# A list scheduler's model of transfers: one serial line, or two queues that share the memory path, with new durations, in a fused graph-attention kernel

## The chip, the cores and the metric

One core of a Trainium2 chip runs the whole problem in one launch. The metric is the device time of that core in microseconds, the median of three runs. Beside it stands one profiled execution, from which all views come.

## The reference

For each of 32 graphs of 512 nodes: a layer norm and a ReLU over the 512 features, two graph-attention layers, and the input added back. Cut to what matters:

```python
h = jnp.maximum(_layernorm(x, axis=-1), 0.0)
def gat_layer(x, mask, W, a_src, a_dst, bias, concat):
    xl = (x @ W).reshape(B, N, H, F)
    asrc = jnp.einsum('bnhf,hf->bnh', xl, a_src)
    adst = jnp.einsum('bnhf,hf->bnh', xl, a_dst)
    e = jax.nn.leaky_relu(asrc[:, :, None, :] + adst[:, None, :, :], NEG_SLOPE)
    e = jnp.where(mask[..., None], e, NEG_INF)
    attn = jax.nn.softmax(e, axis=1)
    out = jnp.einsum('bsdh,bshf->bdhf', attn, xl)
    ...
mask = (adj > 0) | jnp.eye(N, dtype=bool)[None]
h = jax.nn.elu(gat_layer(h, mask, W1, att_src1, att_dst1, b1, concat=True))
return x + gat_layer(h, mask, W2, att_src2, att_dst2, b2, concat=False)
```

Layer 1 has 4 heads of 256 features, layer 2 one head of 512. All matmuls are in float32.

## The kernel before, in words

**Work.** The graphs are pipelined by hand in the main program: while graph i is in its second layer, graph i+1 is in its first, graph i+2 is projected and graph i+3 is loaded. Matrix products of 2 x 2 blocks are made from seven block products in place of eight (`sevens`, `gather1`, `gather2`), so there are block sums on VectorE ahead of them (`hs`, `t`, and sums in place in `ht`, `h1`, `p`) and copies or additions out of PSUM behind each (`minus`, `elu`).

The softmax of a head takes two passes. In the first (`Soft.first`) the scores with destinations on the partitions go through ScalarE (`l<-as,z`), VectorE adds the mask and takes the extreme (`l<-l,mt`), ScalarE takes exponentials and their sum (`l<-l,low`) and a logarithm. `spread` turns the few resulting columns into rows on all partitions, by a small transpose on VectorE and two transfers through DRAM on SyncE: `drr<-rr` and `rr<-drr` (`das<-as` and `as<-das` for the scores themselves). In the second (`Soft.second`) VectorE forms the logits `p<-rr,z`, GpSimd issues two accumulating DMAs that add the mask (`p<-dm`), and ScalarE takes the exponentials (`p<-p,z`). Only then can TensorE gather. The last graph's two late heads use the place of the first weights (`pz`, shown as `w_sb`).

**Transfers.** SyncE issues all plain loads and stores, the broadcasts through DRAM and the transposing DMAs (masks at L527, graph activations at L586). GpSimd issues the accumulating ones at L390, and takes a small power for the layer norm at L546. Each issue waits in its engine's own instruction order.

**Order.** Nothing is emitted while the program is written down. `Program.add` records jobs: engine, cost in microseconds, what they wait for, how to emit them, and for a transfer a size, which is its time on the memory path at full speed. Buffers and PSUM banks are given out in this recording, in program order. `Program.order` then looks for an order of each engine's jobs. `backwards` places the jobs from the end, which gives ranks. `forwards` runs the program in the planner's own time: at each step `next_job` gives the engine that can start first, and of its ready jobs the one of lowest rank. TensorE's jobs are taken from a queue in program order. Twelve rounds of both are made, the best end is kept, and `sooner` then improves stretches of 80 TensorE jobs. At last each job is emitted in the order found. All ScalarE work is issued from line L379, VectorE's from L382, SyncE's from L385, GpSimd's accumulations from L390, matmuls from L396.

**The planner's transfers before.** One line for both queues: a transfer starts when its issue has ended and 0.8 us have passed, or when the one before it has landed; it takes its size, and its readers are released 2.0 us later. No job of SyncE or GpSimd starts while more than 3.5 us (`AHEAD`) of transfers are ahead:

```python
if jobs[j][4] is not None:
    landed = max(landed, t + jobs[j][1] + self.DMA_LEAD) + jobs[j][4]
...
if e in ("SP", "POOL"):
    t = max(t, hold)
```

Of the kernel before, what the change touches and what calls it, by code (L numbers as in the profile page):

```python
# [19 lines left out]
P = 128  # L20
# [24 lines left out]
class Program:  # L45
# [9 lines left out]
    DMA_LEAD, DMA_TAIL, AHEAD = 0.8, 2.0, 3.5  # L55
# [28 lines left out]
    def forwards(self, rank):  # L84

        jobs, after = self.jobs, self.after
        n = len(jobs)
        cause = [None] * n
        left = [len(job[2]) for job in jobs]
        ready_at, start, landed = [0.0] * n, [0.0] * n, 0.0  # L90
        free, soon, ready = defaultdict(float), defaultdict(list), defaultdict(list)
        tensor = deque(j for j in range(n) if jobs[j][0] == "PE")
        for j in range(n):
            if not left[j] and jobs[j][0] != "PE":
                heappush(soon[jobs[j][0]], (0.0, j))
        done = []
        while len(done) < n:
            j, t = self.next_job(rank, free, soon, ready, tensor, left, ready_at, landed - self.AHEAD)
            start[j] = t
            free[jobs[j][0]] = t + jobs[j][1]  # L100
            done.append(j)
            if jobs[j][4] is not None:
                landed = max(landed, t + jobs[j][1] + self.DMA_LEAD) + jobs[j][4]
            for s in after[j]:
                if jobs[j][4] is not None:
                    r = landed + self.DMA_TAIL
                else:
                    r = t + jobs[j][1] + self.latency(j, s)
                if r > ready_at[s]:
                    ready_at[s], cause[s] = r, j  # L110
                left[s] -= 1
                if not left[s] and jobs[s][0] != "PE":
                    heappush(soon[jobs[s][0]], (ready_at[s], s))
        return start, done, cause
# [18 lines left out]
    def backwards(self, rank):  # L133

        jobs = self.jobs
        n = len(jobs)
        left = [len(s) for s in self.after]
        ready_at, start, moving = [0.0] * n, [0.0] * n, 0.0
        free, soon, ready = defaultdict(float), defaultdict(list), defaultdict(list)
        tensor = deque(j for j in reversed(range(n)) if jobs[j][0] == "PE")  # L140
        found = [j for j in range(n) if not left[j]]
        todo = n
        while True:
            for j in found:
                if jobs[j][4] is not None:
                    moving = max(moving, ready_at[j]) + jobs[j][4]
                    ready_at[j] = moving + self.DMA_LEAD
                if jobs[j][0] != "PE":
                    heappush(soon[jobs[j][0]], (ready_at[j], j))
            if not todo:  # L150
                return start
            j, t = self.next_job(rank, free, soon, ready, tensor, left, ready_at)
            start[j] = t
            free[jobs[j][0]] = t + jobs[j][1]
            todo -= 1
            found = []
            for d in jobs[j][2]:
                later = self.DMA_TAIL if jobs[d][4] is not None else self.latency(d, j)
                ready_at[d] = max(ready_at[d], t + jobs[j][1] + later)
                left[d] -= 1  # L160
                if not left[d]:
                    found.append(d)

    def next_job(self, rank, free, soon, ready, tensor, left, ready_at, hold=0.0):

        best = None
        for e in ("PE", "ACT", "DVE", "POOL", "SP"):
            if e == "PE":
                if not tensor or left[tensor[0]]:
                    continue  # L170
                t = max(free[e], ready_at[tensor[0]])
# [6 lines left out]
            if e in ("SP", "POOL"):  # L178
                t = max(t, hold)
            if best is None or t < best[0]:  # L180
                best = (t, e)
        t, e = best
        if e == "PE":
            return tensor.popleft(), t
# [3 lines left out]
        return heappop(ready[e])[1], t  # L188
# [3 lines left out]
    def order(self):  # L192
# [8 lines left out]
        for j in reversed(range(n)):  # L201
            later = self.DMA_LEAD + self.DMA_TAIL + (jobs[j][4] or 0.0)
# [54 lines left out]
def tile_gat(  # L257
# [159 lines left out]
    def weights1():  # L417
        for c in range(2):
            for r in range(2):
                for k in range(KQ):  # L420
# [3 lines left out]
                        0.75, (), [("w1", ix, k)], w1_sb[:, ix, k, :, 2:],  # L424
# [72 lines left out]
    def load(b):  # L497
        XT[b] = []
        for t in range(NT):
            xk, xt = xs.take()  # L500
            dma(0.75, (), [xk], xt, x[b, t * P : (t + 1) * P, :])
            XT[b].append((xk, xt))

    def masks(b):

        for t in range(NT):
            ak, a = adjs.take()
            dma(0.75, (), [ak], a, adj[b, t * P : (t + 1) * P, :])
# [8 lines left out]
            0.5, every, every, nc.vector.tensor_max,  # L517
# [3 lines left out]
        dma(0.45, every, [mk], md.rearrange("p t n -> p (t n)"), m.rearrange("p t n -> p (t n)"))  # L521
        tk, mt = mts.take()

        for t in (0, 2):
# [6 lines left out]
                1.25,  # L531
# [23 lines left out]
    def norm_turn(b, t):  # L555
# [19 lines left out]
        else:  # L575
# [13 lines left out]
                1.27,  # L589
# [16 lines left out]
    class Soft:  # L606
# [7 lines left out]
        def spread(self, v, keys, rows, to, through, n=NT):  # L614
# [8 lines left out]
                0.12, keys, [ok], nc.vector.transpose,  # L623
# [3 lines left out]
                0.03, [ok], [dk], dr[:k].rearrange("k (b j) -> b k j", j=32),  # L627
# [6 lines left out]
                0.18 * rows * n, [dk], [ok], o[:, :rows, : n * P],  # L634
# [77 lines left out]
        def second(self, h):  # L712
# [9 lines left out]
            for d0, d1, rk, rr in self.rr.pop(h):  # L722
# [16 lines left out]
                if not here:  # L739
                    mk, md = MASK[self.b]  # L740
                    for us in (0, 1), (2, 3):
                        keys = p_keys(pk, us)
                        accumulate(
                            2.2, keys + [mk], keys,
# [358 lines left out]
    def residual(b, places=(ts_,) * NT):  # L1103

        XR[b] = []
        for d in range(NT):
# [6 lines left out]
            dma(0.75, [x2_key(b, 0, 0)], halves, xr, x[b, d * P : (d + 1) * P, :])  # L1113
# [29 lines left out]
    def gather2(b, soft, blocks, order=LAST):  # L1143
# [4 lines left out]
        def put(n, u, bk, ps):  # L1148
# [7 lines left out]
            if n == 4 or r == 0 and upper[u[0]] == 0:  # L1156
                upper[u[0]] = -1
                dma(0.75, [xk, xk + (0,), xk + (1,)], (), out[b, d * P : (d + 1) * P, :], xt)
# [10 lines left out]
    def gather2_plain(b, soft):  # L1169
# [3 lines left out]
        for d in range(NT):  # L1173
# [9 lines left out]
            dma(0.75, [xk], (), out[b, d * P : (d + 1) * P, :], xr)  # L1183
# [169 lines left out]
```

## Time and profile before

| | us |
|---|---|
| median of three runs | 2785.93 |
| lowest and highest | 2783.84, 2788.35 |
| span of the profiled execution, first to last instruction | 2778.8 |
| the same execution: TensorE busy | 2746.2 |
| VectorE busy | 2645.4 |
| ScalarE busy | 2304.3 |
| GpSimd busy | 324.7 |
| share of the 16 DMA engines: SyncE's queue, GpSimd's queue | 43.6%, 25.2% |

The span counts from the first to the last instruction; the runs' times also hold what lies around it, so the median stands 7.1 us above this span. "Busy" is time in which an engine's instruction ran; PEld is the loading of weights into TensorE, which overlaps its matmuls. "Idle before" is the time for which an engine stood still ahead of an instruction, put down to the event that ended it. A granted clock of 1.00 is full speed of TensorE. Names read out<-in, without buffer numbers; `mm` is a PSUM bank, `w_sb` a weight (or what later takes its place).

### The profile page before, as it was taken

The page shows a single profiled execution, that of the slowest core. Times are in us where ns is not written, and L with a number is a line of the kernel's source. Part 1 is how long each engine was busy: PE and PEld are TensorE (multiplying, and loading weights), DVE is VectorE, ACT ScalarE, POOL GpSimd, SP SyncE. Part 2 cuts the span into 40 slices and gives each one's busy share as a digit, 9 for nine tenths or more (in the row PEclk, how much of TensorE's full clock was granted, in tenths as well). Part 3 has the DMA queues.
Part 4 walks back from the last instruction along what each step waited for, and adds up shares of the span by engine and source line. Part 5 has one row for each costly group of instructions (what it writes and reads, how often), then busy time and mean ns, then how long its engine had stood idle before and what let it go on. Part 6 is the DMA issues. An engine that isn't in the chain of part 4 may idle for free. (4 is left out here: it accounts for less than half of the span.)

```text
span 2778.8 us, 41571 instructions
## 1 busy us (share of the span) xinstructions
PE 2746.2 (99%) x12520; PEld 2373.9 (85%) x12520; DVE 2645.4 (95%) x6726; ACT 2304.3 (83%) x4870; POOL 324.7 (12%) x356
## 2 busy tenths in 40 slices
PE   7999999999999999999999999999999999999999
PEld 6688888888888888888888888888888888888887
DVE  7999999999999999999999999999999999998997
ACT  5988888889888888888888888888888888887883
POOL 0110111001111101111011101011110111101110
PEclk9999999999999999999999999999999999999999
DMA  7766767667777667676677766777666867678663
GB/s 228 171 176 178 201 174 199 171 175 181 191 194 174 179 165 203 177 186 184 172 192 184 196 168 175 178 189 195 183 175 175 202 166 202 157 189 182 169 158 107
DMA packets 370964, 501.55 MB, mean 180 GB/s; under 512 B 222260, under 2 KB 226868, under 8 KB 370740
## 3 DMA queue, kind: packets, MB, share of 16 engines
q1 hardware_dynamic: 324948, 332.16, 43.6%
q0 software_dynamic: 45792, 166.74, 25.2%
q8 instruction: 100, 1.64, 0.2%
q14 instruction: 124, 1.02, 0.1%
HBM read 315.89 MB, written 51.31 MB: 132 GB/s over the span
## 5 line engine op out<-in xcount | busy, mean ns | idle before, releaser
L396 PE MATMUL mm<-w_sb,hs 128*128 128x257 f32 (+2 forms) x3032 | 688.5, 381 | 4.9 <-DVE hs L382 2.5
L396 PEld LDWEIGHTS mm<-w_sb,hs 128*128 128x128 f32 x3032 | 575.8, 190 | 92.0 <-ACT xl L379 4.6
L390 POOL DMA_DIRECT2D p<-dm x314 | 276.2, 887 | 2346.3 <-DVE p L382 1600.3
L379 ACT ACTIVATE l<-as,z 128x512 f32<-128x512 f32 x640 | 442.8, 721 | 101.9 <-DMA as<-das 96.2
L379 ACT ACTIVATE l<-l,low 128x512 f32<-128x512 f32 x640 | 459.2, 721 | 49.1 <-DVE low L382 46.0
L396 PE MATMUL mm<-w_sb,ht 128*128 128x258 f32 x2112 | 481.4, 382 | 1.9 <-DVE xl L382 1.4
L396 PE MATMUL mm<-p,xl 128*128 128x256 f32 (+1 forms) x1984 | 468.0, 384 | 1.0 <-DVE h L382 0.8
L396 PE MATMUL mm<-w_sb,h 128*128 128x257 f32 x2056 | 467.8, 379 | 0.0
L379 ACT ACTIVATE p<-p,z 128x512 f32<-128x512 f32 (+1 forms) x636 | 427.2, 716 | 42.6 <-DMA p<-dm 28.1
L382 DVE SCALAR_TENSOR_TENSOR p<-rr,z 128x512 f32<-128x512 f32 (+1 forms) x636 | 449.0, 743 | 11.8 <-DMA rr<-drr 11.6
L396 PEld LDWEIGHTS mm<-w_sb,ht 128*128 128x128 f32 x2112 | 400.9, 190 | 61.8 <-DVE xl L382 4.1
L382 DVE CUSTOM_DVE_ANT_1 l<-l,mt 128x512 f32<-128x512 f32 x640 | 429.1, 685 | 12.0 <-ACT l L379 9.5
L396 PEld LDWEIGHTS mm<-w_sb,h 128*128 128x128 f32 x2056 | 389.4, 189 | 57.8 <-issue 0.5
L396 PEld LDWEIGHTS mm<-p,xl 128*128 128x128 f32 x1984 | 377.1, 190 | 61.7 <-issue 5.7
L379 ACT ACTIVATE xl<-mm 128x258 f32<-128x258 f32 (+2 forms) x748 | 279.8, 382 | 70.6 <-PE mm L396 68.7
L379 ACT ACTIVATE h<-mm 128x256 f32<-128x256 f32 x496 | 181.7, 378 | 91.0 <-PE mm L396 88.4
L382 DVE TENSOR_TENSOR xl<-xl,mm 128x258 f32<-128x258 f32 x558 | 222.8, 420 | 29.1 <-PE mm L396 24.3
L379 ACT ACTIVATE xr<-h,b_sb 128x512 f32<-128x512 f32 x248 | 176.7, 721 | 75.7 <-DVE h L382 72.0
L396 PE MATMUL mm<-t,hs 128*128 128x256 f32 x992 | 226.0, 380 | 2.9 <-ACT h L379 2.9
L396 PEld LDWEIGHTS mm<-t,hs 128*128 128x128 f32 x992 | 188.4, 190 | 29.9 <-ACT h L379 4.7
L382 DVE SCALAR_TENSOR_TENSOR h<-h,b_sb,xr 128x512 f32<-128x512 f32 x248 | 182.9, 747 | 3.2 <-ACT xr L379 3.1
L382 DVE TENSOR_TENSOR t<-mm,t 128x256 f32<-128x256 f32 (+1 forms) x424 | 172.8, 419 | 11.7 <-PE mm L396 10.5
(114 smaller groups left out, 3421.8 us busy)
## 6 DMA issues: line engine op xcount, KB each, us to landing
p<-dm POOLq DMA_DIRECT2D x314, 512.0 KB, 5.2
rr<-drr SPq DMA_DIRECT2D x159, 512.0 KB
x<-in_x_dram SPq DMA_DIRECT2D x129, 256.0 KB
adj<-in_adj_dram SPq DMA_DIRECT2D x128, 256.0 KB
as<-das SPq DMA_DIRECT2D x64, 512.0 KB
t<-in_x_dram SPq DMA_DIRECT2D x124, 256.0 KB
out_dram<-t SPq DMA_DIRECT2D x124, 256.0 KB
dm<-m SPq DMA_DIRECT2D x32, 512.0 KB
```

Of the source, the lines that this page charges most:

```text
L379: prog.add("ACT", cost, reads, writes, lambda: nc.scalar.activation(*a, **k))
L382: prog.add("DVE", cost, reads, writes, lambda: f(*a, **k))
L390: lambda: nc.gpsimd.dma_start(to, at, accum_op=OP.add), size,
L396: f(*a, **k)
```

## The change

It is all in the planner and in the numbers that the planner is given. No operation, buffer or wait is added or removed.

- Transfers of SyncE and of GpSimd wait in two queues (`wires`). The first of each moves at speed 1.0 when it is alone. When both move, SyncE's advances at 0.44 and GpSimd's at 0.62; with a transposing DMA (size `TURN`, 0.95) on SyncE, at 0.30 and 0.62.
- The time ahead of a transfer is 0.6 us (SyncE) and 0.75 us (GpSimd), before 0.8; the time after it 1.2 us, before 2.0.
- `AHEAD` stays 3.5 us but counts for each queue by itself (`behind`).
- `next_job` no longer takes the job; `take` does, after `step` has let the transfers that end earlier release their readers.
- Other sizes: mask store `dm<-m` 0.45 to 1.8; broadcasts 0.18 to 0.24 a row of 128; accumulations 2.2 to 2.3; transposes 1.25 and 1.27 to 0.95; small stores 0.03 to 0.2; loads 0.75 to 0.8 or 0.9; stores of the result 0.75 to 0.65. Two costs on VectorE: the diagonal of the mask 0.5 to 0.35, the small transpose 0.12 to 0.13.

The core of the diff:

```diff
-    DMA_LEAD, DMA_TAIL, AHEAD = 0.8, 2.0, 3.5
+    DMA_LEAD, DMA_TAIL, AHEAD = {"SP": 0.6, "POOL": 0.75}, {"SP": 1.2, "POOL": 1.2}, 3.5
+    ALONE = {"SP": 1.0, "POOL": 1.0}
+    SHARED = {0: {"SP": 0.44, "POOL": 0.62}, 1: {"SP": 0.3, "POOL": 0.62}}
+    TURN = 0.95
...
+        wires, now, behind = {"SP": deque(), "POOL": deque()}, 0.0, {"SP": 0.0, "POOL": 0.0}
...
-            j, t = self.next_job(rank, free, soon, ready, tensor, left, ready_at, landed - self.AHEAD)
-            start[j] = t
-            free[jobs[j][0]] = t + jobs[j][1]
-            done.append(j)
-            if jobs[j][4] is not None:
-                landed = max(landed, t + jobs[j][1] + self.DMA_LEAD) + jobs[j][4]
...
+        def step(until):
+
+            nonlocal now
+            busy = [q for q in wires if wires[q] and wires[q][0][1] <= now]
+            speed = self.ALONE
+            if len(busy) == 2:
+                speed = self.SHARED[jobs[wires["SP"][0][0]][4] == self.TURN]
+            event, which = until, None
+            for q in wires:
+                if wires[q]:
+                    j, since, todo = wires[q][0]
+                    t = now + todo / speed[q] if q in busy else since
+                    if t < event:
+                        event, which = t, q
+            for q in busy:
+                wires[q][0][2] -= (event - now) * speed[q]
+                behind[q] -= (event - now) * speed[q]
+            now = event
+            if which in busy:
+                j = wires[which].popleft()[0]
+                release(j, lambda s: event + self.DMA_TAIL[which])
+            return which is not None
+
+        while len(done) < n:
+            hold = {q: now + behind[q] - self.AHEAD for q in wires}
+            found = self.next_job(rank, free, soon, ready, tensor, left, ready_at, hold, now)
+            if step(found[0] if found else float("inf")):
+                continue
+            t, e = found
+            j = self.take(e, t, rank, soon, ready, tensor)
+            start[j] = t
+            free[e] = t + jobs[j][1]
+            done.append(j)
+            if jobs[j][4] is not None:
+                wires[e].append([j, free[e] + self.DMA_LEAD[e], jobs[j][4]])
+                behind[e] += jobs[j][4]
+            else:
+                release(j, lambda s: t + jobs[j][1] + self.latency(j, s))
...
-            if e in ("SP", "POOL"):
-                t = max(t, hold)
+            t = max(t, hold.get(e, 0.0), now)
...
-        dma(0.45, every, [mk], md.rearrange("p t n -> p (t n)"), m.rearrange("p t n -> p (t n)"))
+        dma(1.8, every, [mk], md.rearrange("p t n -> p (t n)"), m.rearrange("p t n -> p (t n)"))
...
-                0.18 * rows * n, [dk], [ok], o[:, :rows, : n * P],
+                0.24 * rows * n, [dk], [ok], o[:, :rows, : n * P],
...
-                            2.2, keys + [mk], keys,
+                            2.3, keys + [mk], keys,
```

## The prediction

> **What bounds the kernel now.** I read the page's busy shares first, then the waits of TensorE, then busy time by stretch of time, then the matmuls in order of time.
>
> ```profile
> span 2778.8 us, 41571 instructions
> PE 2746.2 (99%) x12520; PEld 2373.9 (85%) x12520; DVE 2645.4 (95%) x6726; ACT 2304.3 (83%) x4870; POOL 324.7 (12%) x356
> ```
>
> TensorE is busy all but 2778.8 - 2746.2 = 32.6 us. A busy TensorE is not always a fast one, so I counted records: the seven stretches of 100 us from 200 to 900 us hold 462 or 463 matmuls each, one every 216 ns; nothing is hidden in them. Idle time, by stretch: 11.5 us before the first matmul, 3.8 us after the last (the last addition and store), 5.2 us between 12 and 175 us, 12.1 us after 900 us. These lines show the waits that end last:
>
> ```profile
> PE mm L396 <- ACT x L379: 11.8, 2, 11.5
> PE mm L396 <- DVE hs L382: 3.9, 4, 2.2
> PE mm L396 <- ACT h L379: 3.1, 5, 1.6
> PE mm L396 <- ACT xl L379: 2.4, 4, 1.0
> PE mm L396 <- ACT w_sb L379: 2.2, 1, 2.2
> PE mm L396 <- ACT p L379: 1.7, 2, 1.2
> ```
>
> No line names a DMA: each wait is for a VectorE or ScalarE instruction, and a transfer reaches TensorE only through these. In the next view the columns are length, busy time (count) of PE, PEld, DVE, ACT and POOL, granted clock, DMA share, GB/s:
>
> ```profile
> 45.00:50.00 5.00, 2.52 (x13) 1.72 (x11) 4.44 (x15) 5.00 (x14) 0.00 (x0) 0.99 0.85 257
> 50.00:55.00 5.00, 5.00 (x16) 4.12 (x17) 5.00 (x19) 4.89 (x14) 0.00 (x0) 0.67 0.98 345
> 1060.00:1130.00 70.00, 67.31 (x308) 57.74 (x307) 65.77 (x162) 57.30 (x119) 5.17 (x6) 1.00 0.63 161
> 2500.00:2550.00 50.00, 47.82 (x218) 40.90 (x217) 45.21 (x117) 42.77 (x87) 8.34 (x9) 1.00 0.83 169
> 2680.00:2712.00 32.00, 28.32 (x121) 23.64 (x120) 31.15 (x70) 23.32 (x47) 3.45 (x4) 0.95 0.58 149
> ```
>
> The idle time sits in a few knots: at 45 us TensorE waits for VectorE's block sums `hs` (2.18 us); near 1080 and 1117 to 1120 us; near 2524 us; near 2690 us for the last graphs' `pz`. The second row has a price that idle time doesn't show: after the 2.48 us of idle the clock is 0.67, and 5 x 0.33 = 1.7 us are lost in matmuls at a lower clock.
>
> **What the Trainium skill says.** "Perfetto Trace Analysis", section Identifying the Most-Contended Engine, warns against matmul busy time and wants the share of weight loads: here 85%, with 216 ns between matmuls in each undisturbed stretch, which agrees that TensorE is the bound. "DMA: Bandwidth & Descriptors", section Issuing engines are not separate DMA queues, says that transfers of SyncE and GpSimd run on the same 16 engines and interleave: the page has both queues there (43.6% and 25.2%), so the new model's premise fits the trace. "TensorE: Matmul & The Clock Gate", section What's actually happening, says that an idle window of about 3.4 us halves the clock until a busy one; the trace has 0.67 after a shorter idle time.
>
> **The change, part by part.** It edits no operation, only the list scheduler's model of transfers. TensorE's jobs are taken from a queue in program order in both versions, so its sequence of 2,690 matmul groups and their 2746 us stay. What moves, in the two programs as emitted: 5,264 of 6,020 VectorE instructions have another place, 3,251 of 4,229 on ScalarE, 772 of 1,262 transfers on SyncE, 64 of 350 jobs on GpSimd. So the change can win at most what idle time is left (17.3 us between first and last matmul, some 3 us of lowered clock), and can lose more.
>
> My measure of a move: add the profiled durations of all that now stands ahead of an instruction on its engine, less what stood there before. That is how much later it comes if its engine has no idle time, so for ScalarE (17% idle) it is an upper value. A matmul group is late by this shift less its slack, the time between the end of its last producer and its own start (2.0 us at the median, under 1.04 us for one in ten).
>
> *Start, 44 to 175 us.* The softmax of graph 0 is put ahead of graph 1's projection. Of ScalarE's two copies `ht<-mm` that release TensorE at 45.72 us, the later one has eleven softmax instructions more and one copy less ahead: 4 x 0.61 + 6 x 0.71 + 0.2 - 0.3 = +6.6 us, with ScalarE 100% busy there. The two groups that follow take 1.9 us, so the next group would start at 45.72 + 6.6 + 1.9 = 54.2 us; it waits for `hs<-ht`, 14 places later on VectorE by 5.0 us, so at 49.90 + 5.0 = 54.9 us. Idle time merges with the 2.18 us there: net +5.0 us. For the clock I add 0.5 us (0 if it recovers as before, 1.7 if the longer idle time costs as much again). Graph 2's statistics and activations move from 94-131 us to about 50-68 us: six ScalarE instructions, some 5 us, which fit where ScalarE idled (2.6 us in 75-80 us, 1.5 in 55-60 us and the time that its copies now wait for the late matmuls). On SyncE one mask transpose (1.27 us) now stands ahead of graph 2's loads, and w2's loads follow later; TensorE first reads w2 at 104 us, over 50 us after its load was issued. On GpSimd the power of 1.0 us comes ahead of the first accumulation, which still waits for `rr` at 66 us. With TensorE 5.5 us late and its producers not, the later gaps 0.66 + 0.29 + 0.47 + 1.01 = 2.4 us are covered. Start: +5.5 - 2.4 = **+3.1 us**. If all ScalarE shifts up to 9.9 us (at 98.6 us) bite, +9.9.
>
> *Relief after 900 us.* The producers behind most gaps move ahead: by 3.9 to 6.2 us at 1080 to 1120 us (2.79 us of gaps), 3.1 us at 2524 us (2.18), 2.4 us at 2613 us (0.33), 5.2 us at 2711 us (0.67). At 2690 us the `pz` writes move up 6 to 8 places, and their accumulation, 4.85 us from issue to use, can start sooner (3.01 us of gaps and 0.05 x 32 = 1.6 us of clock). With the small ones at 946 and 2309 us (0.25 + 0.36): 11.2 us. Gaps of 1.08 us at 1798 us and 0.69 at 2437 us stay, as their producers don't move ahead. I take three quarters: **-8.4 us**; bounds -5.5 and -11.2.
>
> *New lateness after 200 us.* In some 17 places a producer moves later than its slack covers; the largest of each place add up to 9.6 us (1.75 at 909 us, 1.7 at 2746 us, else under 1). Idle time of VectorE and ScalarE ahead of them takes part of it: I take 0.4, **+3.8 us**; bounds 0 and 9.6.
>
> *End.* Two residual additions `t<-t,b_sb`, at 2762 and 2763 us before, now stand ahead of the first `p<-rr` of the last graph (2759.18 us), and so wait for their loads in front of it; the last 14 us of matmuls wait for that `p`. VectorE's 0.81 us of idle time at 2758-2759 us takes part of their 2 x 0.6 us, a late load adds: **+1.2 us**, bounds 0 and 3.
>
> Sum: 3.1 - 8.4 + 3.8 + 1.2 = -0.3 us. The profiled span 2778.8 would become 2778.5 us; the median of the runs lies 7.1 us above that span, and I keep this distance: 2785.9 - 0.3 = 2785.6, so **2786 us**.
>
> **Rivals.** *Faster.* The new places are covered, as each of TensorE's neighbours idles for 3 to 17%, and all relief comes: 3.1 - 11.2 + 1.2 = -6.9, 2779 us. For it: producers move ahead by more than the gaps they caused. Against: the delay at 45 us rests on an order that is certain.
>
> *Slower: waits at the head of VectorE's queue.* Its instructions wait in order. One pulled ahead of its transfer stops all behind it, copies out of PSUM and block sums first, and TensorE behind these. Place: once in each graph of the steady part, where loads, `rr` and accumulations are now believed to land at other times. Price: loads of `x` are first used 2.3 us after issue at the earliest and 4.8 us at the lower quartile; one taken at the early end and landing at the other makes 2.5 us, less the median slack of 2.0: 0.5 us x 26 graphs = 13 us, 2799 us. It decides from the point where such a wait exceeds 2 us. For it: VectorE has only 2 to 3 us of idle time in 100. Against: now VectorE waits only 29 us for DMA in the whole span.
>
> *Nothing changes* (the orders are the same) is excluded by the emitted programs.
>
> **Chances.** Some 0.2% (5.6 us) is what a measurement of this kernel can tell from no change: same is 2780.4 to 2791.5 us. Forecast (same) 0.38; faster 0.28; slower 0.34, with the uncovered start (+9.9) counted there. The bounds are -8 (all relief, no new lateness, no loss at the end) and about +17 us; 8 times in 10 the time lies between 2777 and 2800 us.
>
> **What would show it.** TensorE busy 2746 us again; a gap of 6 to 7 us in its matmuls at 45 to 55 us; no gap at 1080 to 1120 and 2524 us, and less at 2690 us; new gaps of a microsecond near 909 and 2746 us. I am wrong if the gap at 45 us is missing, or if idle time is spread over all graphs with VectorE waiting for DMA.

## The result, and the profile after

| | before | changed kernel |
|---|---|---|
| median of 15 runs each, us | 2785.93 | 2791.45 |
| lowest and highest, us | 2775.58, 2793.31 | 2786.52, 2803.51 |
| ratio, 95% interval | | 1.0029 [1.0017, 1.0042] |

The changed kernel is slower by 0.29%: 8.1 us (4.7 to 11.7), if the ratio is taken of 2785.9. (The ratio uses all runs; the two medians alone differ by 5.5 us.) The forecast was 2786 us and no measurable change, which it set at 2780.4 to 2791.5 us. The time lies inside by 0.05 us, and the interval shows a small loss all the same.

First the page of the changed kernel. Its lines of code stand 39 further down: matmuls are L435, ScalarE L418, VectorE L421, SyncE L424, GpSimd L429.

```profile
span 2787.2 us, 41515 instructions
PE 2749.1 (99%) x12520; PEld 2371.6 (85%) x12520; DVE 2643.1 (95%) x6726; ACT 2303.0 (83%) x4870; POOL 323.6 (12%) x356
```

The span is 8.4 us longer: 2.9 us more of busy TensorE and 5.5 us more of idle TensorE (2787.2 - 2749.1 = 38.1, before 32.6). Its waits (total, times, longest):

```profile
PE mm L435 <- ACT x L418: 10.8, 1, 10.8
PE mm L435 <- DVE hs L421: 8.1, 7, 3.4
PE mm L435 <- ACT ht L418: 5.0, 1, 5.0
PE mm L435 <- ACT xl L418: 3.6, 7, 1.0
PE mm L435 <- ACT h L418: 1.7, 2, 1.4
```

Two waits are new in size: one of 5.0 us for ScalarE's `ht`, and `hs`, 8.1 us in place of 3.9. The same five stretches as before (length, busy time of PE, PEld, DVE, ACT, POOL, granted clock, DMA share, GB/s):

```profile
45.00:50.00 5.00, 0.25 (x1) 0.25 (x2) 4.63 (x15) 5.00 (x13) 0.00 (x0) 0.99 0.94 257
50.00:55.00 5.00, 5.00 (x16) 4.07 (x16) 3.97 (x14) 3.13 (x10) 1.46 (x1) 0.67 1.10 297
1060.00:1130.00 70.00, 70.00 (x325) 61.26 (x323) 67.75 (x170) 62.00 (x131) 8.53 (x10) 1.00 0.73 188
2500.00:2550.00 50.00, 50.00 (x233) 43.70 (x232) 48.72 (x127) 42.65 (x85) 7.45 (x8) 1.00 0.81 197
2680.00:2712.00 32.00, 29.88 (x136) 25.23 (x135) 30.05 (x69) 24.89 (x55) 6.91 (x8) 1.00 0.85 215
```

The gap at 45 us is there (5.0 us in one piece, where 6 to 7 were named), the gaps at 1080 to 1120 and at 2524 us are gone, the one at 2690 us has shrunk. Two named signs did not come: TensorE is busy 2749.1 us and not 2746 again, and there are no gaps of a microsecond near 909 and 2746 us. The relief came, and the kernel is slower all the same. So I compared the start of each matmul group in the two traces: how late TensorE is against before. It is 2.4 us late at 228 us, 8.0 at 300, 11.4 at 900, 7.2 at 1125, 8.5 at 1780, 16.8 at 2380, 9.1 at 2712 and 8.4 at the end. What was forecast as relief came (-4.2 and -7.7 us); what was not forecast is the size of the new lateness between, some 19 us where 3.8 were expected.

The largest new gap after the start, 3.4 us at 232 to 235.6 us, shows how it is made. ScalarE's row in the changed kernel's trace (start, length, engine, line, operation; in brackets the idle time ahead and what ended it):

```profile
232.25 1.33 ACT L418 ACTIVATE p<-p,z 128x512 f32<-128x512 f32 x2 [6.50 <-DMA p<-dm]
233.50 1.32 ACT L418 ACTIVATE ht<-x 128x1024 uint16<-128x1024 uint16 x1
```

The exponentials wait 6.5 us for an accumulation. The copy `ht<-x` of the next graph stands behind them in ScalarE's queue; `hs<-ht` on VectorE waits for the copy, and TensorE for `hs`. The accumulation is issued at 220.9 us, with a transposing DMA ahead of it and one beside it. Its line (the last number is the median from issue to landing), and below it that of the same accumulation in the kernel before, which there follows two transposing DMAs:

```profile
p<-dm POOLq DMA_DIRECT2D x1, 512.0 KB, 11.3
```

```profile
p<-dm POOLq DMA_DIRECT2D x1, 512.0 KB, 5.2
```

The Trainium skill, "Perfetto Trace Analysis", section DMA Instruction — SWDGE (GPSIMD), says that such an instruction's end in a profile is the end of writing descriptors, not of moving data; the trace agrees: the instruction takes 0.86 us, the landing comes 10.4 us after its end. Who reads such a trace has to look at landings.

### The profile page after: what moved, and what is told of

Its sections match the earlier page's. It is cut to its first block, busy times and chain, and to the rows that moved or that the text cites. A ratio compares the mean times of both kernels' runs of the same rounds, so it can differ in the third digit from the quotient of the medians.

```text
span 2787.2 us, 41515 instructions
## 1 busy us (share of the span) xinstructions
PE 2749.1 (99%) x12520; PEld 2371.6 (85%) x12520; DVE 2643.1 (95%) x6726; ACT 2303.0 (83%) x4870; POOL 323.6 (12%) x356
## 5 line engine op out<-in xcount | busy, mean ns | idle before, releaser
L435 PE MATMUL mm<-w_sb,hs 128*128 128x257 f32 (+2 forms) x3032 | 690.7, 382 | 10.3 <-DVE hs L421 6.6
L435 PEld LDWEIGHTS mm<-w_sb,hs 128*128 128x128 f32 x3032 | 574.7, 190 | 100.9 <-DVE hs L421 8.4
L429 POOL DMA_DIRECT2D p<-dm x314 | 274.1, 873 | 2289.5 <-DVE p L421 1299.4
L418 ACT ACTIVATE l<-as,z 128x512 f32<-128x512 f32 x640 | 441.5, 718 | 99.5 <-DMA as<-das 86.0
L418 ACT ACTIVATE l<-l,low 128x512 f32<-128x512 f32 x640 | 457.7, 717 | 63.9 <-DVE low L421 61.5
L435 PE MATMUL mm<-w_sb,ht 128*128 128x258 f32 x2112 | 483.9, 383 | 6.3 <-ACT ht L418 5.0
L418 ACT ACTIVATE p<-p,z 128x512 f32<-128x512 f32 (+1 forms) x636 | 430.4, 714 | 59.6 <-DMA p<-dm 44.3
L435 PE MATMUL mm<-w_sb,h 128*128 128x257 f32 x2056 | 467.9, 379 | 0.8 <-DVE w_sb L421 0.8
L421 DVE SCALAR_TENSOR_TENSOR p<-rr,z 128x512 f32<-128x512 f32 (+1 forms) x636 | 450.2, 738 | 16.9 <-DMA rr<-drr 16.8
L435 PE MATMUL mm<-p,xl 128*128 128x256 f32 (+1 forms) x1984 | 466.0, 383 | 0.0
L435 PEld LDWEIGHTS mm<-w_sb,ht 128*128 128x128 f32 x2112 | 402.3, 191 | 67.6 <-ACT ht L418 5.3
L421 DVE CUSTOM_DVE_ANT_1 l<-l,mt 128x512 f32<-128x512 f32 x640 | 424.9, 681 | 22.4 <-ACT l L418 20.9
L435 PEld LDWEIGHTS mm<-w_sb,h 128*128 128x128 f32 x2056 | 389.0, 189 | 59.3 <-DVE w_sb L421 1.2
L435 PEld LDWEIGHTS mm<-p,xl 128*128 128x128 f32 x1984 | 376.3, 190 | 59.4 <-issue 6.2
L418 ACT ACTIVATE xl<-mm 128x258 f32<-128x258 f32 (+2 forms) x748 | 275.7, 380 | 52.4 <-PE mm L435 51.3
L418 ACT ACTIVATE h<-mm 128x256 f32<-128x256 f32 x496 | 179.8, 379 | 101.1 <-PE mm L435 98.8
L421 DVE TENSOR_TENSOR xl<-xl,mm 128x258 f32<-128x258 f32 x558 | 219.6, 414 | 17.9 <-PE mm L435 15.0
L435 PE MATMUL mm<-t,hs 128*128 128x256 f32 x992 | 225.5, 379 | 0.8 <-DVE t L421 0.6
L418 ACT ACTIVATE xr<-h,b_sb 128x512 f32<-128x512 f32 x248 | 177.0, 722 | 55.8 <-DVE h L421 54.8
L435 PEld LDWEIGHTS mm<-t,hs 128*128 128x128 f32 x992 | 188.2, 190 | 27.4 <-DVE t L421 1.0
L421 DVE SCALAR_TENSOR_TENSOR h<-h,b_sb,xr 128x512 f32<-128x512 f32 x248 | 180.8, 739 | 2.5 <-ACT xr L418 2.5
L421 DVE TENSOR_TENSOR t<-mm,t 128x256 f32<-128x256 f32 (+1 forms) x424 | 171.0, 415 | 9.8 <-PE mm L435 9.4
```

Of the source, the lines that this page charges most:

```text
L418: prog.add("ACT", cost, reads, writes, lambda: nc.scalar.activation(*a, **k))
L421: prog.add("DVE", cost, reads, writes, lambda: f(*a, **k))
L429: lambda: nc.gpsimd.dma_start(to, at, accum_op=OP.add), size,
L435: f(*a, **k)
```

## The experiments

Every ratio is to the kernel before, with its 95% interval, from 4 to 22 runs of each kernel; a time in us beside a ratio is worked out from it. Two kinds of kernels were made. One kind changes the planner's numbers and lets it find its order. The other emits a list of the same 14,551 jobs, joined from the two kernels' own lists: up to a group of matmuls in one kernel's order, from there what is left in the other's. At the joints used, the two lists differ in at most two of the jobs already emitted, so a joint itself changes next to nothing. In the kernels with a list, lines of code stand 3 further down than in the changed kernel (matmuls L438, ScalarE L421, VectorE L424, SyncE L427).

| kernel | ratio | 95% interval |
|---|---|---|
| changed kernel | 1.0029 | 1.0017 to 1.0042 |
| early_of_before | 1.0005 | 0.9993 to 1.0017 |
| first_334_of_after | 1.0021 | 1.0005 to 1.0038 |
| two_stretches_of_after | 0.9988 | 0.9975 to 1.0000 |
| three_stretches_of_after | 0.9980 | 0.9968 to 0.9993 |
| the_rest_of_after | 1.0093 | 1.0072 to 1.0114 |
| transposes_ahead | 1.0036 | 1.0026 to 1.0046 |
| both_ahead | 1.0034 | 1.0021 to 1.0047 |
| pool_tail_2 | 1.0023 | 1.0012 to 1.0034 |
| one_line_short_tail | 1.0153 | 1.0133 to 1.0174 |
| tail_2 | 1.0220 | 1.0197 to 1.0243 |
| two_queues_old_durations | 1.0238 | 1.0218 to 1.0259 |
| one_line_new_durations | 1.0260 | 1.0244 to 1.0275 |

### The early order of before (early_of_before)

```diff
     def emit(self):
-        for j in self.order():
+        ...
+        for j in struct.unpack("<%dH" % (len(data) // 2), data):
             self.jobs[j][3]()
```

with the list joined from `[("before", 182), ("after", None)]`.

> The operations are emitted in the order of the kernel before up to the 182nd group of matmuls (216 us), and in the order of the changed kernel from there on. Theory M, new lateness from transfers that land later than the new model plans: the late start of 2.4 us goes, and so do the gaps at 45-60 us; the stalls at 235, 300, 1940, 2031 and 2376 us come back where they were. The time is 2.4 us under the changed kernel, a ratio to before of about 1.002. Rival C, the landings fall by chance and the two orders are equal but for the start: the later stalls don't come back in the same places, and the ratio is 1.000 to 1.001.

Measured 1.0005 [0.9993, 1.0017]. Two stretches of its trace:

```profile
45.00:60.00 15.00, 12.12 (x53) 9.18 (x52) 12.90 (x46) 13.41 (x36) 0.00 (x0) 1.00 1.07 305
230.00:240.00 10.00, 10.00 (x48) 8.74 (x47) 10.00 (x26) 9.56 (x21) 0.86 (x1) 1.00 0.50 132
```

With the early order of before the gap at 45 us is small again, as expected. But the gap at 235 us is gone as well, though the order there is that of the changed kernel: the same accumulation landed after 5.3 us. So 8.1 - 1.4 = 6.7 us of the loss hang on the first 216 us (some 2 to 11, an estimate from the two intervals, so that 2.4 is not excluded by this run alone). Of the later stalls, those expected at 300 and 2031 us came back (at 265 to 268 and 2013 to 2030 us), those at 1940 and 2376 us did not. In their place TensorE waited 2.2 us at 1852 to 1856 us and 2.5 us at 2113 us, where the changed kernel loses only about 0.5 us: rival C is half right.

### Two stretches of the changed order in before (two_stretches_of_after)

```diff
-[("before", 182), ("after", None)]
+[("before", 1007), ("after", 1113), ("before", 2367), ("after", None)]
```

> The order of the kernel before, except for two stretches in the order of the changed kernel: groups 1007 to 1113 (1041 to 1161 us) and everything from group 2367 on (2434 us). In the trace of the changed kernel TensorE made up 3.7 us in the first and 8.4 us in the second against before. Theory M, the relief belongs to the order of these stretches: both come here too, 12.1 us in all, a ratio of 0.9957. Rival L, the changed kernel only caught up there because it was already late and its transfers had had more time: little or nothing is gained, 0.999 to 1.001. Rival C, chance: 1.000, and the gaps at 1080-1120 and 2524-2690 us are partly still there.

Measured 0.9988 [0.9975, 1.0000]: 3.3 us gained (0 to 7), less than the 12.1 of theory M, and not nothing. In the trace 3.0 us were made up at 1090 to 1125 us and 3.0 at 2380 to 2712 us. The trace also has a gap of 4.0 us at 913 to 917 us, in the order of before, where before has none. There two transposes and two accumulations were issued within 3 us, in both kernels. First the two accumulations in this kernel, then in before, with the same instructions in the same order:

```profile
p<-dm POOLq DMA_DIRECT2D x2, 512.0 KB, 12.5
```

```profile
p<-dm POOLq DMA_DIRECT2D x2, 512.0 KB, 6.4
```

So a landing can double without any change of the order, and rival C has a part in every single trace.

### The counterpart (the_rest_of_after)

```diff
-[("before", 182), ("after", None)]
+[("after", 1007), ("before", 1113), ("after", 2367), ("before", None)]
```

> The counterpart: the order of the changed kernel, except that groups 1007 to 1113 (1041 to 1161 us) and everything from group 2367 on (2434 us) have the order of the kernel before. Theory M, the lateness belongs to the order of the other stretches: 10.9 us by 1041 us and 9.6 us more by 2434 us, with nothing made up, 20.5 us in all, a ratio of 1.0074. Rival L, lateness is made up by the transfers whatever the order: about the time of the changed kernel, 1.003. Rival C: 1.001 to 1.003.

Measured 1.0093 [1.0072, 1.0114], 26 us (20 to 32): rival L, 1.003, is excluded, and most of the lateness belongs to the order of the other stretches, as M has it. Not all: of the 37.5 us by which TensorE is late at the end of this trace, 33.5 us were made in the changed order, 10.5 us at 1041 to 1161 us in the order of before, and 6.6 us were made up after 2434 us. (The trace is of the slowest of six runs, 2818 us; their median is 2809.) TensorE's wait for `hs` (total, times, longest):

```profile
PE mm L438 <- DVE hs L424: 25.3, 9, 9.1
```

The start's gap and the gap at 235 us recur (4.5 and 3.2 us), the accumulation again landing after 11.3 us. Two more gaps are long. The one of 9.1 us up to 1102 us lies in the order of before, where before's own trace has 0.3 us: ScalarE's exponentials waited 6.7 us for an accumulation that landed after 11.8 us, then the copy `ht<-x` behind them 4.0 us for a transpose. At the one of 6.9 us up to 2144 us, where early_of_before has 2.5, the copy `ht<-x` waited twice for a transpose, 4.0 and 4.1 us. That it is 26 us rather than the 20.5 expected may come from these.

### A longer margin on both queues (tail_2)

```diff
-    DMA_LEAD, DMA_TAIL, AHEAD = {"SP": 0.6, "POOL": 0.75}, {"SP": 1.2, "POOL": 1.2}, 3.5
+    DMA_LEAD, DMA_TAIL, AHEAD = {"SP": 0.6, "POOL": 0.75}, {"SP": 2.0, "POOL": 2.0}, 3.5
```

> The changed kernel with one number of its model other: from a transfer's end to its release it plans 2.0 us on both queues, as the kernel before did, in place of 1.2 us. Theory M, the loss is too small a margin for landings: ScalarE waits less for accumulations (before 28.1 us over the span, changed 44.3) and TensorE less for ScalarE; the time falls to that of before or under it, a ratio of 0.997 to 1.000. Rival Q, the loss comes of the two queues that share the path, not of the margin: the time stays at that of the changed kernel, 1.003. Rival C: any other order of this kind, within 0.3% of before to either side, with stalls in new places.

Measured 1.0220 [1.0197, 1.0243]: none of the three. Two of ScalarE's waits in the changed kernel, then the same with the longer margin and TensorE's longest wait there:

```profile
ACT xl L418 <- PE mm L435: 51.3, 47, 8.3
ACT p L418 <- DMA p<-dm: 44.3, 40, 6.5
```

```profile
ACT xl L418 <- PE mm L435: 180.1, 75, 9.0
ACT p L418 <- DMA p<-dm: 4.1, 5, 1.3
PE mm L435 <- ACT p L418: 17.8, 22, 2.4
```

The first half of M is right: ScalarE's wait for accumulations falls from 44.3 us to 4.1. The second half is wrong: no time is gained by it, and 61 us are lost. ScalarE now waits 180.1 us for TensorE, at copies `xl`, and TensorE, whose own sequence is fixed, waits 17.8 us for ScalarE's exponentials `p` (1.7 in before). My reading is that an order safe against late landings puts such work too late; no run tests this by itself.

### A longer margin for accumulations alone (pool_tail_2)

```diff
-    DMA_LEAD, DMA_TAIL, AHEAD = {"SP": 0.6, "POOL": 0.75}, {"SP": 1.2, "POOL": 1.2}, 3.5
+    DMA_LEAD, DMA_TAIL, AHEAD = {"SP": 0.6, "POOL": 0.75}, {"SP": 1.2, "POOL": 2.0}, 3.5
```

> The changed kernel with 2.0 us in place of 1.2 us from transfer to release for GpSimd's accumulations alone; SyncE's stay at 1.2. The run with 2.0 on both took 60 us more, and its own plan, as its planner reckons it, already ended 66 us later than that of the changed kernel (2822.6 against 2756.9): the longer latency of SyncE's transfers doesn't fit between the buffers. With 2.0 on GpSimd's queue alone the plan ends at 2759.0. Theory M (late accumulations ahead of ScalarE's other work): ScalarE waits less for accumulations (changed kernel 44.3 us, before 28.1) and TensorE's gap at 235 us goes; ratio to before 0.998 to 1.001. Rival C (late landings fall by chance in either order, transposes as often as accumulations): 1.002 to 1.004, as the changed kernel. Rival Q (the sharing of the path makes the order worse): 1.003.

Measured 1.0023 [1.0012, 1.0034], not told apart from the changed kernel. ScalarE's waits:

```profile
ACT l L418 <- DMA as<-das: 183.3, 55, 6.0
ACT p L418 <- DMA p<-dm: 30.3, 22, 4.4
```

The wait for accumulations falls to 30.3 us, as M expected. But the wait for the broadcast scores rises from 86.0 to 183.3 us, and the time stays. M in this form falls: the accumulations' margin alone is not the cause. Rivals C and Q both gave this time, so the run doesn't part them.

### One part of the change alone (two_queues_old_durations)

```diff
-        dma(1.8, every, [mk], md.rearrange("p t n -> p (t n)"), m.rearrange("p t n -> p (t n)"))
+        dma(0.45, every, [mk], md.rearrange("p t n -> p (t n)"), m.rearrange("p t n -> p (t n)"))
...
-                0.24 * rows * n, [dk], [ok], o[:, :rows, : n * P],
+                0.18 * rows * n, [dk], [ok], o[:, :rows, : n * P],
...
-                            2.3, keys + [mk], keys,
+                            2.2, keys + [mk], keys,
```

and so with all other durations but the transposes', whose size also marks them for the model.

> One part of the change alone: the planner with two queues, its leads and tails as changed, but each transfer's and operation's duration as before. Its own plan ends at 2750.3, 6.6 us before that of the changed kernel. Theory M: the margin is no longer than in the changed kernel, in truth shorter, since a read and an accumulation are planned up to 0.15 us quicker and the mask's write 1.35 us quicker, so late landings cost as much: 1.001 to 1.004. If the durations were what hurts, 0.998 or less.

Measured 1.0238 [1.0218, 1.0259], 66 us, far over what M gave. ScalarE waits 209.1 us for `as<-das` and 73.2 us for `p<-dm`.

### The other part alone (one_line_new_durations)

```diff
-        dma(0.45, every, [mk], md.rearrange("p t n -> p (t n)"), m.rearrange("p t n -> p (t n)"))
+        dma(1.8, every, [mk], md.rearrange("p t n -> p (t n)"), m.rearrange("p t n -> p (t n)"))
...
-                            2.2, keys + [mk], keys,
+                            2.3, keys + [mk], keys,
```

and so with the other durations, in the planner of before.

> The other part alone: the planner with one line of transfers, lead 0.8 and tail 2.0, with the new durations. Its own plan ends at 2802.8, 44 us after that of the kernel before, since transfers that follow each other in one line with longer durations fill it. If the time follows the plan, as it did with 2.0 us on both queues, the ratio is about 1.015 (1.012 to 1.020). If longer durations only order the transfers earlier and the plan's length says nothing, 0.998 to 1.002.

Measured 1.0260 [1.0244, 1.0275], 72 us, over the 1.012 to 1.020 that the plan's length gave. As with tail_2, ScalarE waits long for TensorE (125.8 us, before 68.7).

### The shorter margin alone (one_line_short_tail)

```diff
-    DMA_LEAD, DMA_TAIL, AHEAD = 0.8, 2.0, 3.5
+    DMA_LEAD, DMA_TAIL, AHEAD = 0.7, 1.2, 3.5
```

> The kernel before with lead and tail alone changed, 0.7 and 1.2 us in place of 0.8 and 2.0. Its own plan ends at 2748.0, 11 us earlier than before's. Theory M: the shorter tail alone brings the loss, with no second queue in the model: ScalarE waits more for accumulations and transposes than the 28.1 us and 5.9 us of before, and the 11 us of the plan are not had; ratio 1.000 to 1.004. If the time follows the plan, 0.996. Rival Q: the sharing model is the cause, so there is no loss here, 0.996 to 1.000.

Measured 1.0153 [1.0133, 1.0174], 43 us, far over M's 1.004. ScalarE's waits, then TensorE's:

```profile
ACT l L379 <- DMA as<-das: 191.1, 60, 6.9
ACT p L379 <- DMA p<-dm: 104.7, 75, 4.4
```

```profile
PE mm L396 <- ACT xl L379: 18.0, 19, 2.3
PE mm L396 <- ACT h L379: 16.8, 18, 2.4
```

This is waiting at the head of a queue: ScalarE's first softmax pass is put where its scores have not landed, and the copies `xl` and `h` out of PSUM behind it are what TensorE waits for (2.4 and 3.1 us in before). Q, which put the loss on the shared path alone, falls: a shorter tail does it in the old model.

The five planners beside the two kernels. "Plan" is the end that the kernel's own planner reckons for its order; "over plan" is the median less that; the waits are ScalarE's, for `as`, `p<-dm` and `ht<-x` together, and of `xl` for TensorE:

| kernel | plan, us | over plan | waits for transfers | waits for TensorE | ratio |
|---|---|---|---|---|---|
| one_line_short_tail | 2747.7 | 75.8 | 312.4 | 31.9 | 1.0153 |
| two_queues_old_durations | 2750.3 | 98.0 | 296.8 | 45.8 | 1.0238 |
| before | 2758.9 | 27.0 | 130.2 | 68.7 | 1 |
| changed kernel | 2756.9 | 34.5 | 140.7 | 51.3 | 1.0029 |
| pool_tail_2 | 2759.0 | 30.1 | 232.0 | 39.4 | 1.0023 |
| one_line_new_durations | 2802.8 | 51.9 | 135.9 | 125.8 | 1.0260 |
| tail_2 | 2822.6 | 23.4 | 74.5 | 180.1 | 1.0220 |

A model with too short latencies finds a short plan that isn't kept: ScalarE waits for transfers. One with too long latencies finds a long plan. The change lengthens durations and lets the two queues move side by side with a shorter lead and tail. Either half alone lands on one of these sides and loses 66 to 72 us; together they come back to where before stood. It is a recalibration that nearly cancels. pool_tail_2 waits 232 us and loses 6.4: the sum of the waits is a sign of the side, not a measure of the time. Nor is all of the loss waiting: in the four kernels that lose most TensorE idles 64 to 84 us (before 32.6), and it is also busy 22 to 28 us longer than in before; what makes it busy longer isn't shown.

### The first 334 us of the changed order (first_334_of_after)

```diff
-[("before", 182), ("after", None)]
+[("after", 305), ("before", None)]
```

> The order of the changed kernel up to group 305 of the matmuls (334 us), the order of the kernel before from there on. Theory S, formed after the run with the early order of before came out at 1.0005: the whole loss is made here, 2.4 us by the late start and 5.6 us more at 235 to 275 us, where an accumulation issued among four transposes lands 11.3 us later instead of 5.2 and ScalarE's copy for the next graph stands behind the exponentials that wait for it; what the changed order loses and makes up later comes to about nothing. TensorE is 8.0 us behind at 334 us and stays there: ratio 1.0029 (1.0015 to 1.0043). Rival M, the loss is spread over the later graphs: 1.0010 or less, 2.4 us of the start only. Rival C, late landings by chance: the gap at 235 us is not there.

Measured 1.0021 [1.0005, 1.0038], 5.9 us (1.4 to 10.6): the early order costs most of the loss, by this run as by early_of_before. The two together give about 6 us (some 3 to 10, an estimate from their intervals), more than the 2.4 us of the late start. The mechanism of theory S didn't come: here the accumulation landed after 4.9 us and there is no gap at 235 us. Instead one issued at 86.6 us landed after 7.9 us, and TensorE fell 4.7 us further behind from 85 to 104 us. The late places change, the sum stays similar.

### Two mends (transposes_ahead, both_ahead)

```diff
+# jobs 1071, 1072, 1066, 1067, 1068 (ScalarE's copies, SyncE's transposes) behind job 1070
+tr = move(after, [1071, 1072, 1066, 1067, 1068], 1070)
```

> The order of the changed kernel, with five steps moved up: ScalarE's shift of one tile, its two copies into the transposes' source buffers and SyncE's two transposes of them (issued at 212.3 and 215.4 us; in the kernel before at 206.0 and 209.0) follow at once on the norm of the first, about 206 to 211 us. Theory S: the accumulation issued at 220.9 us meets two transposes fewer and lands after about 5 us, the gaps of 3.6, 0.5, 0.2 and 0.8 us at 235 to 274 us go, all else stays: 5 to 5.6 us less than the changed kernel, ratio 1.0010 (1.0000 to 1.0020). Rival: it is the late start that makes everything late there, the accumulation lands late all the same, and the ratio stays at 1.003.

Measured 1.0036 [1.0026, 1.0046]. The edit did what it was to do at 235 us: the accumulation landed after 4.7 us and the gap shrank from 3.4 us to 0.4. It gained nothing in time. In its trace TensorE lost 3.8 us from 85 to 104 us and 8.0 us from 2000 to 2060 us, where SyncE's queue, the accumulations and ScalarE's copy read:

```profile
2017.96 0.33 SPq L427 DMA_DIRECT2D rr<-drr  x1
2018.35 3.79 SPq L628 DMA_TRANSPOSE x<-adj  x2
```

```profile
p<-dm POOLq DMA_DIRECT2D x2, 512.0 KB, 11.1
```

```profile
2031.35 1.34 ACT L421 ACTIVATE ht<-x 128x1024 uint16<-128x1024 uint16 x1 [6.52 <-DMA x<-adj]
```

Before, at the same place:

```profile
2006.16 1.26 SPq L586 DMA_TRANSPOSE x<-adj  x1
2007.47 0.57 SPq L385 DMA_DIRECT2D rr<-drr  x1
2008.52 1.25 SPq L586 DMA_TRANSPOSE x<-adj  x1
```

In the changed order `rr<-drr`, which waits for its row to land in DRAM, stands at the head of SyncE's queue with both transposes behind it; when it goes, both follow at once, and two accumulations are issued 1.4 and 2.8 us after the first of them. Both kinds then land late. Before had the transposes on either side of `rr<-drr` and issued its accumulations after them, at 2009.7 and 2011.0 us. Here the order tells in every trace: in the five with the changed order the first accumulation landed after 5.2 to 10.5 us and the second after 8.0 to 11.7, in before and the three kernels with its order after 4.7 to 5.4 and 6.5 to 7.5. The five lose 2 to 7 us between 2010 and 2045 us; the other four have no gap there.

```diff
+# ScalarE's four copies ht<-mm (jobs 148, 151, 157, 154), each to just behind its last matmul job
+for c, d in ((148, 147), (151, 150), (157, 156), (154, 153)):
+    tr = move(tr, [c], d)
```

> As the last, and ScalarE's four copies of the first graph's turned tiles (at 49.1 to 52.0 us in the changed kernel, 44.6 to 48.7 before) moved up past the logit work that stands ahead of them, each to just behind its last matmul. Theory S: the gap of 5.6 us at 44 to 50 us shrinks to the 2 to 3 us of before, 2 to 5 us less than the last kernel, ratio 0.9995 (0.9985 to 1.0008): the changed kernel without its two early losses equals the kernel before or is slightly under it. Rival: the logit work that is put back comes due in its turn, and softmax waits at 55 to 130 us take the gain: same as the last kernel.

Measured 1.0034 [1.0021, 1.0047]: no gain, the rival's answer. TensorE's wait at 40 to 70 us, then the stretches:

```profile
PE mm L438 <- DVE hs L424: 7.7, 1, 7.7
```

```profile
40.00:50.00 10.00, 5.83 (x35) 4.93 (x33) 7.61 (x26) 9.42 (x23) 0.00 (x0) 0.96 0.64 141
50.00:55.00 5.00, 1.47 (x4) 1.22 (x5) 4.97 (x17) 3.52 (x11) 1.45 (x1) 0.50 1.02 343
55.00:60.00 5.00, 5.00 (x14) 4.00 (x13) 4.86 (x21) 4.86 (x14) 0.00 (x0) 0.55 1.03 317
```

The wait of 5.0 us for ScalarE's copies is gone, and 7.7 us for `hs` have taken its place: on VectorE `hs<-ht` still stands behind graph 0's logits and graph 2's statistics, as the changed order has it. The longer gap costs more clock as well, 0.50 and 0.55 in place of 0.67.

### The stretches that gain, put into before (three_stretches_of_after)

```diff
-[("before", 182), ("after", None)]
+[("before", 856), ("after", 1113), ("before", 1706), ("after", 1815), ("before", 2367), ("after", None)]
```

> The order of the kernel before, except for three stretches in the order of the changed kernel: groups 856 to 1113 (897 to 1161 us), 1706 to 1815 (1760 to 1869 us), and from 2367 on (2434 us). TensorE made up 4.2 us and 1.3 us and 8.4 us there in the changed kernel's trace; the run with two stretches kept 3.0 and 3.6 us of the first and the last in its trace, and 3.3 us (0 to 7) in its time. If the gains belong to the order: 6 to 9 us, ratio 0.9975 (0.9965 to 0.9988), faster than both kernels. If the late landings by chance outweigh them: 0.9988 to 1.001.

Measured 0.9980 [0.9968, 0.9993], 5.6 us (1.9 to 8.9) under before: faster than both kernels, a median of 2779.15 us. The stretches were chosen by the traces of earlier runs, and the gain held in new runs.

```profile
span 2769.2 us, 41565 instructions
PE 2742.3 (99%) x12520; PEld 2370.6 (86%) x12520; DVE 2641.8 (95%) x6726; ACT 2304.0 (83%) x4870; POOL 322.0 (12%) x356
```

TensorE idles 26.9 us, before 32.6.

## Why the prediction was right or wrong

How late TensorE gets in each stretch, one number for each trace (us against the trace of before), sorted by whose order the kernel has there:

| stretch, us | changed order | order of before |
|---|---|---|
| to 228 | +2.4, +2.2, +7.7 | +0.1, +3.6, +1.0 |
| 228 to 300 | +5.6, +5.5, +1.5, +2.4, +2.4, +2.4 | 0.0, 0.0 |
| 300 to 900 | +3.5, +3.8, +2.1, +2.9, +5.9 | -0.1, -0.1, -0.1 |
| 900 to 1125 | -4.2, -4.3, -4.1, -3.9, -3.8 | +1.8 |
| 1125 to 1780 | +1.3, +4.9, +0.7, +1.3, +3.5 | 0.0, 0.0, 0.1 |
| 1780 to 2380 | +8.3, +16.1, +10.1, +10.4, +13.7 | -1.3, -1.4 |
| 2380 to 2712 | -7.7, -6.7, -3.9, -5.1, -3.0, -6.1 | -2.3, -6.6 |

**The start, +3.1 us: right.** At 228 us three traces with the unmended order are 4.1 us late on average, two of them 2.4 and 2.2 (three with before's order 1.6). The gap at 44 to 51 us recurs in each of them (4.5 to 5.0 us). It ends with ScalarE's copy, where I had `hs`. The clock cost more than the 0.5 us I gave it: beside the 0.67 that before has too, it was 0.83 at 60 to 70 us (an estimate of 10 x 0.17 = 1.7 us), which is part of why TensorE's busy time is 2749.1 us and not 2746 as forecast. One trace, with 7.7, is near the bound of +9.9.

**Relief after 900 us, -8.4 us: right in its places, its size shown only in part.** The places named were those that closed, and two stretches gained 4.1 and 5.4 us on average. That gains belong to the order is shown in time by three_stretches_of_after, which keeps 5.6 us (1.9 to 8.9), some of it (1.6 us by its trace) from the stretch at 1760 to 1869 us, where I expected no relief. In the last stretch much of it may be catching up: kernels with before's order gained 2.3 and 6.6 us there too.

**New lateness after 200 us, +3.8 us with bounds 0 and 9.6: this step failed.** By the traces it is 3.3 + 3.6 + 2.3 + 11.7 = 20.9 us on average over its four stretches, and with before's order there is next to none in these stretches. Elsewhere before's order can be late as well: stretches in which the table's kernels change order are left out of it, and there two_stretches_of_after lost 7.5 us at 900 to 1041 us and the_rest_of_after 10.5 us at 1041 to 1125 us, both in the order of before. The measure that I used, the durations of what now stands ahead on an engine less what stood there, has no term for a transfer's own time. I took each landing as the trace of before had it. But moved transfers meet others: in the changed kernel's trace the accumulation of 220.9 us took 11.3 us and no longer 5.2, the two near 2020 us 6.2 and 8.2 us and no longer 4.7 and 7.3 (10.5 and 11.7 in transposes_ahead). Accumulations that took over 8 us from issue to landing, of 318 in each trace:

| kernel | over 8 us | ratio |
|---|---|---|
| before | 19 | 1 |
| three_stretches_of_after | 20 | 0.9980 |
| first_334_of_after | 21 | 1.0021 |
| two_stretches_of_after | 25 | 0.9988 |
| early_of_before | 25 | 1.0005 |
| both_ahead | 27 | 1.0034 |
| changed kernel | 31 | 1.0029 |
| transposes_ahead | 33 | 1.0036 |
| the_rest_of_after | 38 | 1.0093 |

The count and the time go together, not strictly. And the "17 places" were the wrong places: I named 909 and 2746 us, where 0.2 us and nothing was lost; the lateness sits at 235 to 275 us, at 600 to 670 us and from 1860 to 2380 us.

**The end, +1.2 us: wrong in sign, small.** TensorE is 9.1 us late at 2712 us and 8.4 at the end.

**The distance of 7.1 us from span to median: wrong.** The changed kernel's profiled execution took 2789.0 us with a span of 2787.2, so 1.8 us lie around a span, and before's profiled execution took about 2780.6 us (an estimate, 2778.8 + 1.8): it was a quick one. I took a part of the spread for a constant. Since I kept the distance on both sides, the difference wasn't touched by it; but all the lateness above is counted against a quick trace, and so is too large by up to 5 us.

**The sum.** 4.1 - 4.1 - 5.4 + 20.9 = 15.5 us by the traces, 8.1 (4.7 to 11.7) by the times. The quick trace of before explains up to 5 of the difference; the rest is the spread of single traces, and I can't divide it further. By the times, the early order makes about 6 us of the loss, and what follows comes to about nothing, gains and losses together. That the time is in the forecast's range is in part luck: the sum gave -0.3 us where 8.1 were measured, with a term for new lateness of 3.8 us where the traces show 20.9, and the range ends 0.05 us above the median.

**The rivals.** The slower one had the right kind, a transfer that lands late holding the head of an in-order queue, with a total that is too high (2799 us), and it named VectorE alone: VectorE's wait for `rr` went from 11.6 to 16.8 us, ScalarE's for `p<-dm` from 28.1 to 44.3, and near 2020 us it is SyncE's queue. The faster one failed by its premise that all new places are covered. What I named as the sign of being wrong, idle time over all graphs, didn't come: it sits in a few places.

Two of my theories after the result fell too: the margin for accumulations (pool_tail_2), and the pile of transposes at 212 to 222 us as the cause of the early loss (first_334_of_after, transposes_ahead). Shown is that the early order costs about 6 us (3 to 10) and that late landings behind in-order queues make the gaps that were looked into. That these gaps add up to the loss is not shown: the two kernels in which the gap at 235 us was mended were no faster. Which landing is late differs between kernels that have the same order at that place. What in the early order makes them likelier is open beyond the start's 2 to 4 us.

## What to carry to other kernels

When a scheduler's model is changed, look at what its parts do alone: here each lost 1.5 to 2.6% and together 0.3%, so the old numbers had been balanced against the old model's faults. A sum over moved instructions needs a term for transfers: for each one that moves, ask what it now flies beside, and what is queued behind its reader. And where single traces differ by 5 us without a change, take from a trace the place and the cause of a loss, and its size from many runs; pieces of two orders can be joined and timed.

## What the runs showed of the hardware

Accumulating DMAs of 512 KB took 4.1 to 15.4 us from issue to landing. I counted over nine traces how many transposing DMAs ended their issue from 3 us before to 4 us after an accumulation's issue: with none, a median of 5.2 us and 7.8 at the 95th percentile (1,996 of them); with one 6.2 and 9.4 (613); with two 6.1 and 11.2 (252). Only the slow tail is sure: counted by the starts of the transposes' issues, the medians don't part (5.5, 5.2 and 5.7 us), the 95th percentiles still do (8.3, 9.0 and 11.5). With two such transposes, and another accumulation in the 3.5 us before, it was 8.0 and 12.5 (76). The same two accumulations, in kernels with the same order up to there, took 12.5 us in one trace and 6.4 in another (the median of the two). I had not expected so wide a step.
